# First attention of a sixteen-stage network: TensorE's order in groups of four units

## The chip, the cores and the metric

The kernel runs on one core of a Trainium2 chip. The metric is the device time of one execution in microseconds; lower is better. The core's engines run side by side, each with its own queue of instructions in a fixed order: TensorE (PE, matrix multiplications, with its weight loads shown as PEld), VectorE (DVE), ScalarE (ACT), GpSimd (POOL) and SyncE (SP, which issues most transfers). An instruction starts when those ahead of it in its queue and those whose results or buffers it needs are done. TensorE writes only to PSUM; VectorE and ScalarE copy from there into SBUF.

## The reference

The network has sixteen stages; each adds its result to x, of shape (4, 512, 128), after a layer normalisation. The change touches only the first, an attention with 16 heads of width 64:

```python
x = x + _L0_attn_a_ref(_layernorm(x), q_w, q_b, k_w, k_b, v_w, v_b, l_w, l_b)

def _L0_attn_a_ref(x, ...):
    q = jnp.einsum('bsd,hpd->bhsp', x, q_w) + q_b          # likewise k and v
    scores = jnp.einsum('bhqp,bhkp->bhqk', q, k) / jnp.sqrt(jnp.float32(P))   # P = 64
    attn = jax.nn.softmax(scores, axis=2)                  # over the queries, not the keys
    ctx = jnp.einsum('bhqk,bhkp->bqhp', attn, v)
    return ctx.reshape(B, S, H * P) @ l_w.T + l_b
```

The softmax runs over the queries. So the denominator belongs to a key, and can be put into that key's row of v.

## The kernel before

All data are fp32 and x stays in SBUF. The first stage, `L0a`, works through 4 batches of 8 head pairs, 32 groups `m`. A group has four *units* `n = 4m + j`, one for each block of 128 keys, with both heads of the pair.

For a unit, `scores(n)` (line 526) lets TensorE multiply 128 keys by 512 queries for each of the two heads (64 rows of the array each) into a PSUM tile of two banks, from a ring named "sc" of two such tiles. VectorE takes the two maxima `mx` over the queries (line 533); ScalarE takes two exponentials `e` with their sums (line 538), into a ring of nine SBUF buffers. After the fourth unit of a group VectorE takes the reciprocal `z` (line 547), and GpSimd multiplies v by it into `vz` (line 549). `sums(n)` (line 556) multiplies a unit's `e` by `vz` and adds it up over the four units of its group in a bank of the ring "ctx"; after the fourth, VectorE copies it out as `ct` (line 571).

The projections of a group each take one bank of a ring named "mm", which has two banks: `query(m)` (copied out, with bias and scale, by VectorE, line 507), `key(m)` (copied out with its bias by ScalarE, line 514), `value(b, c)` (one eighth of a batch's v; copied out with its bias by VectorE, line 524). `output(b, j)` (line 576) multiplies the eight finished `ct` of a batch by the last weights, also into "mm", and VectorE adds it to x and takes the moments for the next normalisation. The rings together fill the eight banks of PSUM: four for "sc", two for "mm", two for "ctx".

The order on TensorE is written out: every multiplication is pinned to program order. VectorE's and ScalarE's instructions stand in the order in which the same program names them. The loop at line 605 goes by pairs of units: scores of two units, sums of the two units six earlier (`LAG = 6`), then what `Plan` has set for this pair. That is query and key of the next group at one pair of each group, one value of the next batch at the other, and an output behind it four times a batch. `Plan.at(n, f, ...)` puts a call on step n, and `Plan.run(n)` makes the calls of that step in the order in which they were put there.

A short notation for blocks of TensorE's work: S, the scores of two units; C, the sums of two; Q, K, V, one projection each; O, one output. Before, a group is S C Q K, S C V, with O behind V where there is one.

Of the kernel before, what the change touches and what calls it, by code (L numbers as in the profile page):

```python
# [19 lines left out]
B, S, D = 4, 512, 128  # L20
NT = B * S
NC = NT // P
CB = S // P
# [251 lines left out]
class Net:  # L275
# [206 lines left out]
    def L0a(self):  # L482


        nc, tc = self.nc, self.tc
        LAG = 6
        with (
            tc.tile_pool(name="l0a_s", bufs=1) as sp,
            tc.tile_pool(name="l0a_r", bufs=3) as rp,
# [6 lines left out]
            plan = Plan()  # L496
# [29 lines left out]
            def scores(n):  # L526
                m, j = divmod(n, CB)
                sc = pp.tile([P, 2, S], F32, tag="sc", name="ps_s")
                for hh in range(2):
                    r = slice(64 * hh, 64 * hh + 64)  # L530
                    self.mm(sc[:, hh], k[m][r, j * P : j * P + P], q[m][r, :], pin=True)
                mx = rp.tile([P, 2], F32, tag="mx", name="mx", bufs=4)
                nc.vector.tensor_reduce(mx, sc, AX.X, ALU.max, negate=True)  # L533
                if j == 0:
                    z[m] = rp.tile([P, CB, 2], F32, tag="z", name="z")
                es[n] = rp.tile([P, 2, S], F32, tag="e", name="e", bufs=9)
                for hh in range(2):
                    nc.scalar.activation(  # L538
                        es[n][:, hh],
                        sc[:, hh],  # L540
                        AF.Exp,
                        bias=mx[:, hh : hh + 1],
                        accum_out=z[m][:, j, hh : hh + 1],
                    )
                if j == CB - 1:
                    b, pr = divmod(m, 8)
                    nc.vector.reciprocal(z[m], z[m])  # L547
                    vz[m] = rp.tile([P, CB, 2, 64], F32, tag="vz", name="vz")
                    nc.gpsimd.tensor_tensor(  # L549
                        vz[m],  # L550
                        v[b][:, :, pr * P : pr * P + P].rearrange("p j (h d) -> p j h d", h=2),
                        z[m].unsqueeze(3).to_broadcast([P, CB, 2, 64]),
                        ALU.mult,
                    )

            def sums(n):
                m, j = divmod(n, CB)
                if j == 0:
                    pc[m] = pp.tile([P, S], F32, tag="ctx", name="ps_c")
                for hh in range(2):  # L560
                    self.mm(
                        pc[m][64 * hh : 64 * hh + 64, :],
                        vz[m][:, j, hh],
                        es[n][:, hh],
                        start=j == 0,
                        stop=j == CB - 1,
                        pin=True,
                    )
                if j == CB - 1:
                    ct[m] = rp.tile([P, S], F32, tag="ct", name="ct", bufs=13)  # L570
                    nc.vector.tensor_copy(ct[m], pc[m])
                    if m % 8 == 7:
                        for i in range(CB):
                            plan.at(n + LAG + 1 + 4 * i, output, m // 8, i)

            def output(b, j):
                po = pp.tile([P, D], F32, tag="mm", name="ps_o")
# [16 lines left out]
            for c in range(8):  # L594
                value(0, c)
            for m in range(1, 8 * B):
                plan.at(4 * m - 4, query, m)
                plan.at(4 * m - 3, key, m)
            for b in range(1, B):
                for c in range(8):  # L600
                    plan.at(32 * (b - 1) + 4 * c + 2, value, b, c)
            for b in range(B):
                plan.at(32 * b + 16, self.bias_x, b, "a0_lb")

            for n in range(0, 32 * B + LAG + 16, 2):
                if n < 32 * B:
                    scores(n)
                    scores(n + 1)
                if 0 <= n - LAG < 32 * B:
                    sums(n - LAG)  # L610
                    sums(n - LAG + 1)
                plan.run(n)
                plan.run(n + 1)

    def experts(
        self, pools, NH, last, weighed, n, wide, gates, hidden, w2, rest, bias=False
# [7 lines left out]
        sp, rp, pp, dp = pools  # L624
        LAG = 12
        off = 64 if bias else 0
# [2292 lines left out]
```

## Time and profile before

| what | value |
|---|---|
| time, median of 3 runs | 2432.72 us (2425.2 to 2433.19) |
| profiled execution, from its first to its last instruction | 2427.6 us |
| TensorE busy over the span | 2172.0 us, 89% |
| first scores of the stage to its outputs' start | 26.7 to 380.8 us |
| TensorE busy from 26 to 381 us | 352.1 of 355 us |
| VectorE, ScalarE, GpSimd busy there | 229.4, 200.9, 33.3 us |
| granted TensorE clock there | 1.00 |

The page gives no other time of the profiled execution than its span. A line of the timeline begins with the start and the duration in microseconds; then come engine, line of the kernel, operation, output and inputs, shapes, and how many instructions are merged. In brackets stand the engine's idle time just before and what ended it. A matrix multiplication in fp32 shows as two MATMUL rows. The rows of TensorE overlap, since multiplications are pipelined, so a block's price is read from its start to the start of the next block.

### The profile page before, as it was taken

How to read it: one execution, taken by the hardware profiler on the slowest of the kernel's cores; microseconds unless marked ns; L12 is line 12 of the kernel's file. 1: busy time of each engine (PE TensorE's matmuls, PEld its weight loads, DVE VectorE, ACT ScalarE, POOL GpSimd, SP SyncE). 2: the span in 40 equal slices, each digit the busy share in tenths (PEclk: the TensorE clock that was granted, in tenths of full speed). 3: DMA queues.
4: the chain of work that ended last, by engine and by line, in shares of the span. 5: the costliest groups of instructions: out<-in, count | busy, mean ns of one | idle time of the engine just before them, and what ended most of it. 6: DMA issues, size and time to landing. Idle time of an engine off the chain costs nothing.

```text
span 2427.6 us, 32659 instructions
## 1 busy us (share of the span) xinstructions
PE 2172.0 (89%) x11639; PEld 1029.5 (42%) x11639; DVE 1727.7 (71%) x3413; ACT 1284.5 (53%) x2550; POOL 609.7 (25%) x443
## 2 busy tenths in 40 slices
PE   7999999999999998899876889888869998888868
PEld 2343334643334443568534446542214666422213
DVE  6666666589987775656465674678997657678995
ACT  4555555279845555343442454566655445467643
POOL 1100100010000001021153410038872014147871
PEclk9999999999899998999866989998979999988989
DMA  3000001300000000410200014334552520034550
GB/s 143 1 1 1 1 1 48 94 1 2 2 1 2 1 1 1 106 36 2 107 1 1 0 42 91 69 121 140 157 145 54 91 49 2 1 113 146 158 153 20
DMA packets 68882, 127.79 MB, mean 53 GB/s; under 512 B 9329, under 2 KB 29297, under 8 KB 68081
## 3 DMA queue, kind: packets, MB, share of 16 engines
q1 hardware_dynamic: 68720, 125.71, 19.2%
q8 instruction: 92, 1.51, 0.3%
q14 instruction: 70, 0.57, 0.1%
HBM read 119.91 MB, written 5.64 MB: 52 GB/s over the span
## 4 chain that ended last, share of the span: by engine, by line
PE 25%; DVE 12%; issue 8%; ACT 5%; DMA 1%; POOL 1%; SPq 0%; POOLq 0%; DVEq 0%; ACTq 0%
PE ps_o L346 6%; PE ps L346 4%; DVE hc L2361 3%; PE ps_x L346 2%; PE ps_g L346 2%; PE ps_du L346 2%; DVE ps_du L2356 2%; PE ps_y L346 1%; PE ps_h L346 1%; PE ps_s L346 1%; DMA wt<-dram 1%; DVE xn L393 1%; PE ps_d L346 1%; PE ps_tr L351 1%; ACT da L2342 1%
## 5 line engine op out<-in xcount | busy, mean ns | idle before, releaser
L2366 POOL TENSOR_TENSOR hc<-hc,cr 128x1024 f32<-128x1024 f32 x126 | 297.3, 2360 | 117.6 <-DVE hc L2361 111.6
L2361 DVE TENSOR_TENSOR_SCAN hc<-da,ps_du 128x1024 f32<-128x1024 f32 x128 | 290.9, 2274 | 0.0
L346 PE MATMUL ps_s<-k,q 32*128 32x512 f32 (+3 forms) x1088 | 277.5, 593 | 10.7 <-DVE mx L839 7.9
L538 ACT ACTIVATE e<-ps_s,mx 128x512 f32<-128x512 f32 x256 | 172.4, 685 | 139.5 <-DVE mx L533 132.9
L346 PE MATMUL ps_du<-du,spread 64*128 64x512 f32 x512 | 163.6, 711 | 63.3 <-DVE hc L2361 63.1
L925 DVE TENSOR_REDUCE nm<-ps_s 128x1 f32<-128x512 f32 x256 | 160.2, 681 | 60.3 <-PE ps_s L346 58.9
L2342 ACT ACTIVATE da<-da,am 128x512 f32<-128x512 f32 x248 | 165.7, 715 | 65.0 <-DMA da<-dram 49.0
L346 PE MATMUL ps<-xT,w_L2f 128*128 128x512 f32 (+1 forms) x416 | 193.4, 612 | 0.0
L1011 ACT ACTIVATE e<-ps_st 128x512 f32<-128x512 f32 x256 | 135.4, 602 | 93.8 <-PE ps_s L346 82.4
L533 DVE TENSOR_REDUCE mx<-ps_s 128x2 f32<-128x1024 f32 x128 | 150.9, 1218 | 43.9 <-PE ps_s L346 43.6
L2356 DVE TENSOR_TENSOR ps_du<-ps_du,br 128x1024 f32<-128x1024 f32 x128 | 154.8, 1210 | 30.5 <-PE ps_du L346 30.4
L346 PE MATMUL ps_st<-q,k 32*128 32x512 f32 x512 | 165.3, 625 | 1.7 <-DVE q L942 1.0
L850 ACT ACTIVATE e<-e,mx 128x512 f32<-128x512 f32 (+3 forms) x256 | 140.2, 549 | 19.3 <-DVE mx L839 18.6
L346 PEld LDWEIGHTS ps_s<-k,q 32*128 32x128 f32 x1088 | 99.2, 192 | 105.7 <-DVE mx L839 49.6
L346 PE MATMUL ps_s<-q,k 64*128 64x512 f32 x512 | 129.1, 618 | 2.2 <-ACT e L538 1.7
L346 PE MATMUL ps_c<-e,vz 128*64 128x512 f32 x512 | 123.5, 604 | 0.8 <-POOL vz L549 0.8
L1933 DVE SCALAR_TENSOR_TENSOR t<-ps,w_L2f,t 128x512 f32<-128x512 f32 (+1 forms) x104 | 76.6, 746 | 61.8 <-PE ps L346 38.9
L346 PEld LDWEIGHTS ps_du<-du,spread 64*128 64x128 f32 x512 | 46.2, 205 | 173.9 <-issue 113.8
L346 PEld LDWEIGHTS ps<-xT,w_L2f 128*128 128x128 f32 (+1 forms) x416 | 75.5, 190 | 95.8 <-issue 75.2
L549 POOL TENSOR_TENSOR vz<-v,z 128x512 f32<-128x512 f32 x32 | 33.3, 1042 | 323.1 <-DVE z L547 294.1
L839 DVE CUSTOM_DVE_ANT_0 e<-ps_s,tri 128x512 f32<-128x512 f32 (+3 forms) x256 | 109.5, 483 | 6.1 <-PE ps_s L346 6.1
L659 DVE TENSOR_TENSOR hc<-hc,wt 128x1024 f32<-128x1024 f32 x80 | 94.7, 1188 | 23.6 <-ACT hc L1936 12.1
(499 smaller groups left out, 4179.5 us busy)
## 6 DMA issues: line engine op xcount, KB each, us to landing
da<-dram SPq DMA_DIRECT2D x124, 256.0 KB
da<-dram SPq DMA_DIRECT2D x124, 255.5 KB
wt<-dram SPq DMA_DIRECT2D x144, 128.0 KB
wt<-dram SPq DMA_DIRECT2D x32, 256.0 KB
dram<-dl SPq DMA_DIRECT2D x16, 256.0 KB
wt<-dram SPq DMA_DIRECT2D x16, 224.0 KB
wt<-dram SPq DMA_DIRECT2D x16, 192.0 KB
wt<-dram SPq DMA_DIRECT2D x16, 160.0 KB
```

The lines of the kernel that those rows point to most:

```text
L346: i = self.nc.tensor.matmul(out, lhsT, rhs, start=start, stop=stop)
L533: nc.vector.tensor_reduce(mx, sc, AX.X, ALU.max, negate=True)
L538: nc.scalar.activation(es[n][:, hh], sc[:, hh], AF.Exp, bias=mx[:, hh : hh + 1], accum_out=z[m][:, j, hh : hh + 1],)
L659: nc.vector.tensor_tensor(h, h, wt[b, k][:, r:e], ALU.mult)
L839: red = nc.vector.tensor_tensor_reduce(e[:, i, :w], sc[i][:, :w], tri[:, S - w :], -1.0, BIG, ALU.add, ALU.min, mx[:, i : i + 1],)
L850: nc.scalar.activation(e[:, i, :w], e[:, i, :w], AF.Exp, bias=mx[:, i : i + 1], scale=-1.0, accum_out=z[:, i : i + 1],)
L925: nc.vector.tensor_reduce(nm[:, j, i, 9:10], sc, AX.X, ALU.max, negate=True)
L1011: keep(nc.scalar.activation(es_[n][:, i], sc, AF.Exp))
L2342: nc.scalar.activation(da[n][:, t, t:], src[:, t:], AF.Exp, scale=am[:, at : at + 1])
L2356: keep(nc.vector.tensor_tensor(dx[n], dx[n], br, ALU.mult))
L2361: keep(nc.vector.tensor_tensor_scan(h, a, x, 0.0, ALU.mult, ALU.add))
L2366: keep(nc.gpsimd.tensor_tensor(hc[n], hc[n], cr, ALU.mult))
```

## The change

The loop now goes by groups of four units. Each round issues scores of two units, then everything planned for this group (query and key of the next group, a value, an output, in this order), then scores of the other two units, then the sums of all four units of the group before. The plan's steps are counted in groups; `LAG` is gone.

```diff
-        LAG = 6
...
                     if m % 8 == 7:
                         for i in range(CB):
-                            plan.at(n + LAG + 1 + 4 * i, output, m // 8, i)
+                            plan.at(m + 2 + i, output, m // 8, i)
...
             for m in range(1, 8 * B):
-                plan.at(4 * m - 4, query, m)
-                plan.at(4 * m - 3, key, m)
+                plan.at(m - 1, query, m)
+                plan.at(m - 1, key, m)
             for b in range(1, B):
                 for c in range(8):
-                    plan.at(32 * (b - 1) + 4 * c + 2, value, b, c)
+                    plan.at(8 * (b - 1) + c, value, b, c)
             for b in range(B):
-                plan.at(32 * b + 16, self.bias_x, b, "a0_lb")
-
-            for n in range(0, 32 * B + LAG + 16, 2):
-                if n < 32 * B:
-                    scores(n)
-                    scores(n + 1)
-                if 0 <= n - LAG < 32 * B:
-                    sums(n - LAG)
-                    sums(n - LAG + 1)
-                plan.run(n)
-                plan.run(n + 1)
+                plan.at(8 * b + 4, self.bias_x, b, "a0_lb")
+
+            for m in range(8 * B + CB + 1):
+                if m < 8 * B:
+                    scores(4 * m)
+                    scores(4 * m + 1)
+                plan.run(m)
+                if m < 8 * B:
+                    scores(4 * m + 2)
+                    scores(4 * m + 3)
+                if 0 < m <= 8 * B:
+                    for j in range(CB):
+                        sums(4 * m - 4 + j)
```

A group is now S, Q K V, S, C C, with O behind V where there is one. No operation is added, dropped or resized. The values of the last three batches fall into groups 0 to 23; outputs fall into groups 9 to 12, 17 to 20 and 25 to 28, and the last four stand behind the loop's last sums.

## The prediction

> **What bounds the kernel now.** I read the page's busy rows and slices first, then the timeline of TensorE over one group of four units, then VectorE and ScalarE at the stage's start, then the two places of the stage where TensorE waits. From the page:
>
> ```profile
> PE 2172.0 (89%) x11639; PEld 1029.5 (42%) x11639; DVE 1727.7 (71%) x3413; ACT 1284.5 (53%) x2550; POOL 609.7 (25%) x443
> PE   7999999999999998899876889888869998888868
> PEclk9999999999899998999866989998979999988989
> ```
>
> TensorE leads. The changed stage runs from 26.7 us (first scores) to 380.8 us (last outputs); PE is at 9 there, and the table of stretches gives a granted clock of 1.00 for all of it, with DVE 229 and ACT 201 busy of 355 us. So only TensorE's order and its waits can move this stage. One group, on TensorE alone:
>
> ```profile
> 203.52 1.02 PE L346 MATMUL ps_k<-xT,w_L0a 128*128 128x512 f32 x2
> 204.47 1.99 PE L346 MATMUL ps_s<-q,k 64*128 64x512 f32 x8
> 206.39 1.94 PE L346 MATMUL ps_c<-e,vz 128*64 128x512 f32 x8
> 208.26 1.12 PE L346 MATMUL ps_v<-w_L0a,xT 128*128 128x512 f32 x2
> 209.31 1.99 PE L346 MATMUL ps_s<-q,k 64*128 64x512 f32 x8
> 211.23 1.94 PE L346 MATMUL ps_c<-e,vz 128*64 128x512 f32 x8
> 213.10 1.12 PE L346 MATMUL ps_q<-xT,w_L0a 128*128 128x512 f32 x2
> ```
>
> Start to start, S (scores of two units) costs 1.92, C (sums of two) 1.86, V 1.05, Q+K 1.91 us: 10.54 a group and no wait. What stands behind a score block is read at the stage's first S (start 26.73):
>
> ```profile
> 27.91 2.35 DVE L533 TENSOR_REDUCE mx<-ps_s 128x2 f32<-128x1024 f32 x2 [0.38 <-PE ps_s L346]
> 30.18 0.74 DVE L507 TENSOR_SCALAR q<-ps_q,w_L0a 128x512 f32<-128x512 f32 x1
> 31.17 0.69 ACT L538 ACTIVATE e<-ps_s,mx 128x512 f32<-128x512 f32 x1
> 31.83 0.70 ACT L514 ACTIVATE k<-ps_k,w_L0a 128x512 f32<-128x512 f32 x1
> ```
>
> The copy of q out of PSUM comes behind both maxima and ends 4.19 us after S began (30.92); the copy of k comes behind four exponentials and ends 5.80 after (32.53). Both are in PSUM ring "mm", which has two banks. What a TensorE block does that needs a bank of this ring still being copied is seen with the eight V at the start:
>
> ```profile
> 21.11 0.69 DVE L524 TENSOR_TENSOR v<-ps_v,rows 128x512 f32<-128x512 f32 x1 [0.35 <-PE ps_v L346]
> 21.86 0.30 PEld L346 LDWEIGHTS ps_v<-w_L0a,xT 128*128 128x128 f32 x2 [0.75 <-DVE v L524]
> ```
>
> It starts 0.06 us after the copy ends (21.80). Score banks ("sc", two) come free late too, where nothing stands between two S:
>
> ```profile
> 295.93 1.99 PE L346 MATMUL ps_s<-q,k 64*128 64x512 f32 x8
> 299.92 1.13 PE L346 MATMUL ps_s<-q,k 64*128 64x512 f32 x4
> 301.26 1.13 PE L346 MATMUL ps_s<-q,k 64*128 64x512 f32 x4 [0.21 <-ACT e L538]
> 302.32 1.94 PE L346 MATMUL ps_c<-e,vz 128*64 128x512 f32 x8
> ```
>
> That is 3.99 and 5.33 us after the earlier S began, 6.39 to the next block. Last, a block of four units' sums and the outputs (O):
>
> ```profile
> 309.89 2.05 PE L346 MATMUL ps_o<-w_L0a,ct 128*128 128x128 f32 x16
> 311.87 1.99 PE L346 MATMUL ps_s<-q,k 64*128 64x512 f32 x8
> 377.26 3.65 PE L346 MATMUL ps_c<-e,vz 128*64 128x512 f32 x16 [0.78 <-POOL vz L549]
> 380.84 7.41 PE L346 MATMUL ps_o<-w_L0a,ct 128*128 128x128 f32 x64
> ```
>
> O alone costs 1.98, four units' sums 3.58 (two C cost 3.72).
>
> **The change, part by part.** No matmul, copy or transfer is added or dropped. Blocks per group become S, Q K V (and O), S, C4. In the built kernel's order ScalarE, POOL and SP have the same sequence as before. VectorE has each pair of maxima still ahead of q's copy; V's copy moves ahead of the second pair, the copy of the context behind it.
>
> *Fewer switches of block.* C4 for two C saves 0.14. Q, K and V in one run, if nothing waits, save 0.20: V's 1.05 becomes the 0.85 of two 0.43 us passes (V to V at the start, 19.95 to 20.81). Together 0.34 a group with V.
>
> *New wait 1: V on q's copy.* Q, K and V take three turns of a ring of two, so V needs q's bank. Count from S. Q starts at 1.92, K at 2.88, V could at 3.73. q's copy ends at 4.19, so V starts at 4.25 and, having started from a standstill, costs 1.05: the second S starts at 5.30. Its banks have been free since 3.99 and (second unit, due at 6.26) 5.33. Then S 1.92 and C4 3.58: the group takes **10.80** against 10.54, +0.26. Queued behind V are the second S, C4 and everything after; nothing else of TensorE can pass.
>
> *New wait 2: O on k's copy.* Where an output follows V, it needs k's bank: 5.80 + 0.06 = 5.86. O 1.98, S 1.92, C4 3.58: **13.34**. Before, such a group took 12.32 (134.93 to 147.25, K to K): +1.02. Where it follows K without V (last batch), it waits for q's copy, 4.25 + 1.98 + 1.92 + 3.58 = **11.73** against 11.47 (315.65 to 327.12): +0.26.
>
> *Groups with neither V nor O.* S, then S on freed banks, next block at 6.39, C4 to **9.97**; before 10.18 (294.01 to 304.19): −0.21.
>
> *Start.* First sums come, as before, after the scores of eight units, but no C fills the gaps. First S 26.73; V waits to 30.98, second S 32.03; third S waits for score banks (32.03 + 3.99 = 36.02, second unit 37.36), ends 38.42; Q K; q's copy, behind the reciprocal (37.42) and two maxima, ends 40.51; V 40.57; fourth S 41.62; C4 43.54; third group at 47.12. Before, its S began at 44.08: +3.0.
>
> *End.* From S of the last group to the outputs: S, S on freed banks and C4 end at 9.97, but the last sums need vz, which before came 5.49 after the last unit's scores began (371.77 to 377.26): 5.33 + 5.49 + 3.58 = 14.40 against 14.71 (366.13 to 380.84): −0.3.
>
> *Edits costed at nothing.* V's copy now stands before the second pair of maxima: ready 1.16 after V began (5.41), done 6.10, maxima due at 6.48; without that 0.38 us of cover up to 0.69 a group would be lost. Reciprocal and copy of the context end 0.12 + 0.69 after C4, 0.37 before the next maxima are due (S + 1.18). vz is ready some 2 us into the next group and used at 7.2. At most eight units wait for their sums; of the nine e buffers, the one written next had its sums a group earlier. The four bias additions on POOL ran at 15.8 to 20.8 us, ahead of the stage's loop, and still can.
>
> *Sum.* Groups 2 to 30: 14 with V × 0.26 = +3.6; 8 with V and O × 1.02 = +8.2; 4 with O × 0.26 = +1.0; 3 plain × −0.21 = −0.6; start +3.0; end −0.3: **+14.9 us**. Bounds of the two prices that no row shows in this place: the start from a standstill costs V between 0.85 and 1.05 (22 × 0.2 = 4.4 less at most), and a wait costs from 0.06 to 0.2 us beyond the copy (the idle shown at 301.26) for 30 waits, 4 more. So +10.5 to +19; I take the rows' own starts, since V after a wait is shown at 1.05.
>
> The profiled execution spans 2427.6 us and no row lies outside it; the shown runs are 2425.2, 2432.7 and 2433.2, their median 5.1 above. 2432.7 + 14.9 = 2447.6. About 0.5% (12.2 us) is what a measurement of this kernel can tell from no change.
>
> [...]
>
> **The rivals.** *Not slower: the ring does not bind.* If q's copy ended by 3.67 after S, 0.52 earlier than shown (ahead of one maximum), and k's likewise, only the switches would count: 22 × −0.34 = −7.5; O without V −0.36 × 4 = −1.4; plain −0.6; start +2.0; end −0.3: −7.8, 2425. For it: TensorE has shown no wait for this ring in steady groups. Against: Q, K and V never came together there, and VectorE's order keeps both maxima ahead.
>
> *Smaller: O does not wait for k.* If ScalarE does k's copy before the second unit's exponentials, O runs on from V: 4.25 + 2.83 (V to S, 218.80 to 221.63) + 5.50 = 12.58, +0.26 in place of +1.02: +8.8, 2441. Against: the built order and the row at 31.83.
>
> *Larger: VectorE falls behind.* It does 4 × 1.21 + 0.75 + 0.69 + 0.69 + 0.19 = 7.2 us of each 10.8, but the margins are 0.37 and 0.38. If one is missed by 0.4 a group in 26 groups: +10 more, 2458. Against: both are counted from rows of the same order.
>
> **How the numbers follow.** Forecast 0.68 (own range 2443 to 2452), ring not binding 0.06, smaller 0.13, larger 0.13. Slower by over 0.5% (above 2444.9): the larger case and all but 0.05 of the forecast, 0.76. Faster (below 2420.6) needs more than the −7.8 of the first rival, a piece of it with run noise: 0.03. The rest, 0.21, is the same. The range leaves out the first rival and the top of the larger: 2437 to 2458.
>
> **What would show it.** Right: V's weight load waits for DVE q some 0.5 us, O's for ACT k some 0.5 us; group periods 10.8, 13.3, 11.7, 10.0; the stage's outputs begin near 396; the rest of the kernel unmoved. Wrong: Q, K, V in 2.8 us without a wait, periods near 10.2; or second S or maxima late by more than the sum has, for score banks or VectorE.

## The result, and the profile after

The changed kernel takes 2443.56 us (median of 5 runs, 2441.04 to 2446.07), the kernel before 2432.62 us beside it (5 runs): ratio 1.0055, 95% interval 1.0038 to 1.0072. By the medians it is slower by 10.9 us, by the ratio by 13.4 us: the ratio is not the quotient of the two medians, which is 1.0045, and the means of the five runs give 1.0058. Measured again beside the experiments it was slower by more, 1.0086 (1.0072 to 1.0101); both are taken up below. The profiled execution took 2442.09 us, with a span of 2440.0 us. One kernel below, with half of the first values later and two banks, was profiled in a run of 3645.18 us at a mean granted clock of 0.665, where its other four runs had 0.929 or more, so no profile of it is read and its time is the median of those four.

The page of the changed kernel, its busy times, and TensorE's slices:

```profile
PE 2165.6 (89%) x11639; PEld 1029.5 (42%) x11639; DVE 1728.1 (71%) x3413; ACT 1283.0 (53%) x2550; POOL 610.3 (25%) x443
...
PE   7999999999899998899885889988868998888868
```

Busy times and counts of instructions are nearly those of before, and the slices of the first 400 us read as before, one 7 and then 9. Nothing on this page tells that the stage got longer; a loss of half a microsecond in each group of eleven is lost in rounding. The timeline shows it: one group with a value, and one with a value and an output, on TensorE and with the copy that is waited for.

```profile
104.56 1.99 PE L346 MATMUL ps_s<-q,k 64*128 64x512 f32 x8
...
108.01 0.74 DVE L506 TENSOR_SCALAR q<-ps_q,w_L0a 128x512 f32<-128x512 f32 x1
108.80 1.13 PE L346 MATMUL ps_v<-w_L0a,xT 128*128 128x512 f32 x2 [0.34 <-DVE q L506]
...
115.36 1.99 PE L346 MATMUL ps_s<-q,k 64*128 64x512 f32 x8
...
126.16 1.99 PE L346 MATMUL ps_s<-q,k 64*128 64x512 f32 x8
...
130.41 1.12 PE L346 MATMUL ps_v<-w_L0a,xT 128*128 128x512 f32 x2 [0.34 <-DVE q L506]
131.33 0.70 ACT L513 ACTIVATE k<-ps_k,w_L0a 128x512 f32<-128x512 f32 x1
132.08 2.05 PE L346 MATMUL ps_o<-w_L0a,ct 128*128 128x128 f32 x16 [0.55 <-ACT k L513]
```

(Two lines fewer stand in the changed file, so the copy of q is L506 here, that of k L513, the exponentials L537.) V begins 4.24 us after its group's first S instead of 3.73, O 5.92 us after it, each 0.05 us behind the end of the copy. The waits of TensorE from 26 to 400 us, with total, number and longest:

```profile
PE ps_v L346 <- DVE q L506: 7.9, 23, 0.3
...
PE ps_o L346 <- ACT k L513: 4.3, 8, 0.5
PE ps_o L346 <- DVE q L506: 1.4, 4, 0.3
```

Before, 24 weight loads of V waited for the maxima (19.4 us in all, from 26 to 381 us), behind other work, and no matmul waited for a copy of q or k. Now 23 V wait for q's copy, 8 O for k's and 4 O for q's.

| part of the stage, us | before | after | difference | predicted |
|---|---|---|---|---|
| group with V | 10.54 | 10.80 | +0.26 (14 groups) | +0.26 |
| group with V and O | 12.32 | 13.40 | +1.08 (8) | +1.02 |
| group with O alone | 11.47 | 11.73 | +0.26 (4) | +0.26 |
| group with neither | 10.18 | 9.98 | −0.20 (3) | −0.21 |
| third group to last group's start | 322.05 | 335.27 | +13.2 | +12.2 |
| first S to the third group's start | 17.35 | 23.09 | +5.7 | +3.0 |
| last group's start to the outputs | 14.71 | 14.41 | −0.3 | −0.3 |
| stage, first S to outputs | 354.1 | 372.8 | +18.7 | +14.9 |
| outputs' successor (first `ps_g`) to the span's end | 2036.7 | 2029.7 | −7.0 | 0 |

The stage lost more than was predicted, by the start; the rest of the kernel, which the change does not touch, came out shorter in this one profile. The start, on TensorE, and the clock in a piece of it (after the stretch: its length, then busy time and number of instructions for PE, PEld, DVE, ACT and POOL, the granted clock, DMA):

```profile
36.70 1.13 PE L346 MATMUL ps_s<-q,k 64*128 64x512 f32 x4 [1.95 <-ACT e L537]
...
40.05 2.07 PE L346 MATMUL ps_q<-xT,w_L0a 128*128 128x512 f32 x2
```

```profile
36.00:38.00 2.00, 1.13 (x4) 0.30 (x4) 0.29 (x1) 1.99 (x6) 0.00 (x0) 0.93 0.00 0
38.00:40.00 2.00, 1.96 (x4) 0.51 (x4) 1.30 (x2) 0.64 (x2) 1.04 (x1) 0.50 0.00 0
...
44.00:46.00 2.00, 2.00 (x6) 0.49 (x6) 0.69 (x1) 0.55 (x1) 0.00 (x0) 0.86 0.00 0
```

The idle of 1.95 us before the third S is the predicted wait for the score banks. What was not predicted is that after it TensorE works at half its clock for a while: Q takes 2.07 in place of 1.13 us. The two stretches left out, from 40 to 44 us, have 0.50 as well, so the time at half clock follows from the clock column, with 1.00 and 0.50 taken as its only values: 2 × 2.00 × (1 − 0.93) + 2.00 + 2.00 + 2.00 + 2 × 2.00 × (1 − 0.86) = 6.84 us.

### The profile page after: what moved, and what is told of

Same layout as the page of the kernel before. It is cut to its first block, busy times and chain, and to the rows that moved or that the text cites. A ratio compares the mean times of both kernels' runs of the same rounds, so it can differ in the third digit from the quotient of the medians.

```text
span 2440.0 us, 32604 instructions
## 1 busy us (share of the span) xinstructions
PE 2165.6 (89%) x11639; PEld 1029.5 (42%) x11639; DVE 1728.1 (71%) x3413; ACT 1283.0 (53%) x2550; POOL 610.3 (25%) x443
## 4 chain that ended last, share of the span: by engine, by line
PE 25%; DVE 12%; issue 8%; ACT 4%; DMA 1%; POOL 1%; SPq 0%; POOLq 0%; DVEq 0%; ACTq 0%
PE ps_o L346 6%; PE ps L346 5%; DVE hc L2363 3%; PE ps_x L346 2%; PE ps_g L346 2%; DVE ps_du L2358 2%; PE ps_du L346 2%; PE ps_h L346 1%; PE ps_s L346 1%; PE ps_y L346 1%; DVE xn L393 1%; DMA wt<-dram 1%; PE ps_d L346 1%; PE ps_tr L351 1%; DVE ln_st L374 1%
## 5 line engine op out<-in xcount | busy, mean ns | idle before, releaser
L537 ACT ACTIVATE e<-ps_s,mx 128x512 f32<-128x512 f32 x256 | 172.6, 686 | 176.1 <-DVE mx L532 176.1
L346 PE MATMUL ps_c<-e,vz 128*64 128x512 f32 x512 | 116.9, 598 | 0.8 <-POOL vz L548 0.8
L661 DVE TENSOR_TENSOR hc<-hc,wt 128x1024 f32<-128x1024 f32 x80 | 94.7, 1189 | 25.6 <-ACT hc L1938 12.2
```

Source lines behind the costliest of these rows:

```text
L346: i = self.nc.tensor.matmul(out, lhsT, rhs, start=start, stop=stop)
L537: nc.scalar.activation(es[n][:, hh], sc[:, hh], AF.Exp, bias=mx[:, hh : hh + 1], accum_out=z[m][:, j, hh : hh + 1],)
L661: nc.vector.tensor_tensor(h, h, wt[b, k][:, r:e], ALU.mult)
```

## The experiments

Theory: the two banks of ring "mm" make V wait for q's copy and O for k's, and that is the whole steady loss. Rivals: it is the order itself (switches of block, VectorE, the score banks), or the start.

### A third bank for the projections, with the new order

The third bank is taken from "ctx", which keeps one, so that the three rings take eight banks as before.

```diff
-            tc.tile_pool(name="l0a_p", bufs=2, space=PSUM) as pp,
+            tc.tile_pool(name="l0a_p", bufs=3, space=PSUM) as pp,
...
-                sc = pp.tile([P, 2, S], F32, tag="sc", name="ps_s")
+                sc = pp.tile([P, 2, S], F32, tag="sc", name="ps_s", bufs=2)
...
-                    pc[m] = pp.tile([P, S], F32, tag="ctx", name="ps_c")
+                    pc[m] = pp.tile([P, S], F32, tag="ctx", name="ps_c", bufs=1)
```

> The changed kernel with the eight PSUM banks divided otherwise: three for the projections' ring "mm" and one for "ctx", in place of two and two. Nothing else differs. Theory (V and O wait for the copies of q and k because the ring has two banks): no wait before V or O; groups with V take 1.92 + 2.77 + 1.92 + 3.58 = 10.2 us (10.80 in the changed kernel), with V and O 12.05 (13.40), with O alone 11.1 (11.73), plain ones 9.98 as before; 14 x 0.6 + 8 x 1.35 + 4 x 0.6 + 1.2 at the start = 22 us less than the changed kernel, near 2421 us, 0.995 of the kernel before. Rival (the time was lost to VectorE's maxima, to score banks or to the start): periods stay 10.8 and 13.4, near 2443 us. If one bank for ctx binds, the sums' first multiplication waits for DVE ct and the groups grow.

Measured: 2426.22 us (11 runs) against 2430.81 (25), ratio 0.9981 (0.9970 to 0.9992). A group with V and O on TensorE:

```profile
130.61 1.99 PE L346 MATMUL ps_s<-q,k 64*128 64x512 f32 x8
...
134.35 1.02 PE L346 MATMUL ps_v<-w_L0a,xT 128*128 128x512 f32 x2
135.21 1.95 PE L346 MATMUL ps_o<-w_L0a,ct 128*128 128x128 f32 x16
...
142.58 1.99 PE L346 MATMUL ps_s<-q,k 64*128 64x512 f32 x8
```

V and O follow without a gap: V costs 0.86 us with O behind it (134.35 to 135.21), the group takes 11.97 in place of 13.40, and a group with V alone 10.19 in place of 10.80. With the waits gone the new order is the faster one, by the switches that it saves: the stage takes 348.4 us against 354.1 before. The steady loss is the ring's. The whole gains less than expected (2421 us, 0.995): from the third group to the last it takes 312.9 us in place of 322.05 before, but the start still costs 3.6 us more than before, a spell of half clock among it. The price of the single "ctx" bank is one wait of 0.89 us for `ct` at the very end, where 0.78 us for `vz` stood.

### The same rings with the old order

The same three lines, put into the kernel before.

> The kernel before with the same division of PSUM (three banks for "mm", one for "ctx"). Theory: in the old order no steady group waits for this ring, so groups stay at 10.54 and 12.32 us and the time within 0.1% (about 1 us less at most, from the eight values at the start). Rival (the third bank is worth something in any order): the old order gains some of the 22 us too.

Measured: 2432.56 us, ratio 1.0003 (0.9992 to 1.0015); groups of 10.54 and 12.32 us as before, stage 354.2 us. A third bank by itself is worth nothing. In the old order no matmul of the steady groups waits for a bank of "mm"; only order and ring together decide.

### The output in the other ring

To part the two waits, O alone is moved out of "mm"; V stays there.

```diff
-                po = pp.tile([P, D], F32, tag="mm", name="ps_o")
+                po = pp.tile([P, D], F32, tag="ctx", name="ps_o")
```

> The changed kernel, with the outputs' banks taken from the ring "ctx" in place of "mm"; V still waits for q. Theory (two separate waits): V's weight load still waits for DVE q, O no longer for ACT k: groups with V and O 12.6 us (13.40), with O alone 11.1 (11.73), with V 10.80 as they are; 8 x 0.8 + 4 x 0.6 = 9 us less than the changed kernel, near 2434 us. Rival (O is dear for itself, or waits for something else): 13.4 stays, 2443 us.

Measured: 2437.98 us (8 runs), ratio 1.0023 (1.0010 to 1.0036), and on TensorE:

```profile
124.30 1.99 PE L346 MATMUL ps_s<-q,k 64*128 64x512 f32 x8
...
128.55 1.12 PE L346 MATMUL ps_v<-w_L0a,xT 128*128 128x512 f32 x2 [0.34 <-DVE q L506]
129.51 1.95 PE L346 MATMUL ps_o<-w_L0a,ct 128*128 128x128 f32 x16
...
136.89 1.99 PE L346 MATMUL ps_s<-q,k 64*128 64x512 f32 x8
```

V waits as in the changed kernel, O no more. The group takes 12.59 us, which is the 12.58 that the rival "O does not wait for k" had; groups with V alone stay at 10.80, and a group with O alone falls from 11.73 to 11.12, as expected. The time is 4 us above the 2434 expected. So O's wait is worth 13.40 − 12.59 = 0.81 us in each of 8 groups, V's 12.59 − 11.97 = 0.62 in each of 22, its costlier start included.

### Key before query

> The changed kernel with key ahead of query in each group, so that V needs the bank of k, whose copy ends 1.6 us later than q's. Theory (the ring): V starts at 5.86 after the first scores in place of 4.25; groups with V 12.4 us (10.80), with V and O 14.2 (13.40, O then has q's bank, long free), with O alone 13.3 (11.73); 14 x 1.6 + 8 x 0.8 + 4 x 1.6 + 3 at the start = 38 us more, near 2482 us. Rival (V's delay has another cause than the copy two places earlier): no change, 2443 us.

```diff
-                plan.at(m - 1, query, m)
                 plan.at(m - 1, key, m)
+                plan.at(m - 1, query, m)
```

Measured: 2453.32 us, ratio 1.0092 (1.0076 to 1.0108). The first group with V after the start; ScalarE and TensorE in order of time:

```profile
46.26 1.99 PE L346 MATMUL ps_s<-q,k 64*128 64x512 f32 x8
...
50.04 0.69 ACT L513 ACTIVATE k<-ps_k,w_L0a 128x512 f32<-128x512 f32 x1
50.61 0.69 ACT L537 ACTIVATE e<-ps_s,mx 128x512 f32<-128x512 f32 x1
50.77 1.12 PE L346 MATMUL ps_v<-w_L0a,xT 128*128 128x512 f32 x2 [0.61 <-ACT k L513]
...
57.33 1.99 PE L346 MATMUL ps_s<-q,k 64*128 64x512 f32 x8
```

The direction holds: the projection that comes first names the copy that V waits for, here k's. The size does not: 2482 us was expected. The group takes 11.07 us (later ones mostly 11.13) where about 12.4 was expected, because ScalarE's order moved with the edit: the copy of k now stands ahead of the second unit's two exponentials instead of behind them. It begins 3.78 us after S, and V 0.04 us after its end. A group with V and O falls to 12.92 us, since O no longer waits. In turn the second unit's exponentials come later, and a group with neither V nor O grows to 10.56 us, on a longer wait for a score bank. The edit changed two engines' orders, not one, which the expectation had missed. The program still names all four exponentials ahead of `key`: only TensorE's multiplications are pinned, and unlike what the section on the kernel before says, ScalarE does not always follow the program's order. What chose this order is not shown.

### Half of the first values later

The start's gap of 1.95 us has nothing to fill it. Here four of the eight values that stand ahead of the first S are moved behind the second scores of the first two groups.

```diff
-            for c in range(8):
-                value(0, c)
+            fill = Plan()
+            for c in range(0, 8, 2):
+                value(0, c)
+                fill.at(c // 4, value, 0, c + 1)
...
                     scores(4 * m + 3)
+                fill.run(m)
```

> The changed kernel, with four of the first batch's eight values (those of pairs 4 to 7, needed from group 4 on) taken out of the run ahead of the loop and put behind the second scores of groups 0 and 1, two each. They fill the 1.95 us in which TensorE stands before group 1. Theory (the start costs more than its waits, since TensorE's granted clock halves after this gap): the gap shrinks to some 0.2 us, and with it the spell of clock 0.50 (37.9 to 44.7 us in the changed kernel, some 2.7 us of time) goes; third group 2 us earlier by the gap and up to 2.7 more by the clock; groups after it as in the changed kernel (10.80, 13.40). Rival (the spell comes at that time of the kernel whatever TensorE does): only the 2 us, and clock 0.50 still there near 38 to 45 us.

Measured: 2444.85 us (4 runs), ratio 1.0064 (1.0049 to 1.0078), beside 1.0086 for the changed kernel on the same chip, so about 2429.1 × 0.0022 = 5.3 us less, with intervals that overlap. That the half clock goes with the gap, which this run was to test, is not shown by it; what the moved values do to the start is read from the next kernel.

### Three banks and the late values

Both edits together.

> Ring of three and late values together, meant as the version that beats both kernels: periods 10.2, 12.0, 11.1, 9.98 as with the ring of three, and 2 us less at the start, with a half-clock spell up to 4: some 2423 us, 0.996 to 0.997 of the kernel before. Rival: the late values' copies on VectorE delay the maxima of groups 0 and 1, and the start gains nothing: 0.998.

Measured: 2423.40 us (12 runs) against 2429.10 (17), ratio 0.9971 (0.9959 to 0.9983): faster than both kernels, as expected (0.996 to 0.997). From the kernel with three banks alone (0.9981) it can't be told apart by time. Its start:

```profile
29.40 1.98 PE L346 MATMUL ps_v<-w_L0a,xT 128*128 128x512 f32 x4
31.42 1.13 PE L346 MATMUL ps_s<-q,k 64*128 64x512 f32 x4
```

The two values take the place of the 1.95 us of idle, and the clock stays at 1.00 from 26 to 50 us; that it stays there because the idle is gone is not shown by one profile, since it stayed full behind the idle too (see the changed kernel again, below). From first S (22.79) to the third group (44.00) it takes 21.21 us and contains four values more, two by two at 1.92 us (38.50 to 40.42 for the second two); so 17.4 for the rest, the 17.35 of before.

### The value beside query and key, in the old order

The other half of the change: the kernel before, with its pairs and its sums in between, but V at the pair of Q and K.

```diff
-                    plan.at(32 * (b - 1) + 4 * c + 2, value, b, c)
+                    plan.at(32 * (b - 1) + 4 * c + 1, value, b, c)
```

> The kernel before, with its loop by pairs, and one part of the change alone: the value moved from its own pair to behind query and key, so that groups are S C Q K V, S C. Theory (V, where it stood, also covered the wait for score banks): V waits some 0.16 us for q's copy, saves one switch (0.2), and the two S with only C between them now wait for exponentials, 3.99 and 5.33 us after the earlier S: groups with V 11.3 us (10.54), the 8 with an output in that place little changed (12.3), 14 x 0.7 = 10 us more, near 2441 us. Rival (only the number of switches counts): 0.2 less a group, near 2428 us.

Measured: 2442.63 us, ratio 1.0058 (1.0044 to 1.0072). A group on TensorE, and the score banks' waits in the stage:

```profile
40.23 1.99 PE L346 MATMUL ps_s<-q,k 64*128 64x512 f32 x8
...
45.50 1.13 PE L346 MATMUL ps_s<-q,k 64*128 64x512 f32 x4 [0.21 <-ACT e L538]
...
49.39 1.02 PE L346 MATMUL ps_k<-xT,w_L0a 128*128 128x512 f32 x2
50.40 1.12 PE L346 MATMUL ps_v<-w_L0a,xT 128*128 128x512 f32 x2
51.46 1.99 PE L346 MATMUL ps_s<-q,k 64*128 64x512 f32 x8
```

```profile
PE ps_s L346 <- ACT e L538: 6.2, 21, 1.9
```

Q, K and V come together here too, and V's wait all but goes. With C ahead of Q the maxima are done, and what VectorE's copy of q waits for is Q itself (29 times, 10.3 us in all); Q ends at 49.55 us. V, whose weight loads wait for that copy (24 times, 20.0 us in all), begins 1.01 us after K (49.39 to 50.40) in place of 0.86 in a run without a wait: 0.15 us late, as expected (0.16), and not the 0.51 of the changed kernel. The loss is another one. With V gone from between the two S, only C is left there, the score banks are late, and the group takes 11.23 us here and 11.29 in most others (11.3 expected), against 10.54. Of these 0.75 us, 0.69 stand at the two S (85.42 to 91.81 less C's 1.86 and two S at 1.92), and 0.06 at Q, K and V. A group with V and O takes 12.58 us where 12.3 was expected. So V's old place was cover for the score banks, and what makes V wait long in the changed kernel is not that the three are together but that they come straight behind S, with q's copy behind two maxima.

### The changed kernel again

> The changed kernel unaltered, once more beside these on the same chip: between the two profiles its first stage is longer by 18.7 us and its whole by 12.4. Theory (the rest of the kernel is the same, and its time varies with the spells of half clock): the stage repeats within 3 us, the rest of the kernel after the first ps_g lies anywhere in the 2030 to 2047 us that the profiles showed so far, and the ratio to the kernel before is 1.006 to 1.008. Rival (the later stages really run faster behind the changed stage): rest again near 2030 and ratio 1.005 or less.

Measured: 2448.58 us (2446.03 to 2454.27), ratio 1.0086 (1.0072 to 1.0101), groups of the same lengths as in its first profile. The start, and a pair of scores near the stage's end:

```profile
35.40 1.13 PE L346 MATMUL ps_s<-q,k 64*128 64x512 f32 x4 [1.95 <-ACT e L537]
...
385.70 3.42 PE L346 MATMUL ps_s<-q,k 64*128 64x512 f32 x8 [2.01 <-ACT e L537]
```

The same idle of 1.95 us, and the clock stays full (1.00 from 26 to 50 us; Q takes 1.12): first S (26.16) to third group takes 20.26 us, +2.9 against before. This time the half clock comes behind the idle of 2.01 us in the last group, whose scores take 3.42 us:

```profile
386.00:388.00 2.00, 2.00 (x6) 0.50 (x4) 0.77 (x1) 0.98 (x4) 0.00 (x0) 0.58 0.00 0
388.00:390.00 2.00, 2.00 (x8) 0.43 (x6) 1.29 (x2) 1.45 (x4) 0.00 (x0) 0.56 0.00 0
```

From the last group's S (381.70) to the outputs (397.06) it takes 15.36 us, 0.65 more than before in place of 0.3 less. The stage takes 370.9 us: 2.9 + 13.2 + 0.65 = 16.8 more than before.

## Why the prediction was right

2447.6 us was predicted, +14.9, with bounds of +10.5 and +19; measured were +10.9 and, the second time, +19.5 by the medians, one on each side. The terms of the steady groups, 12.2 of the 14.9 us (13.2 measured), were right in mechanism and nearly in size. That the first total lies as near as it does is partly luck: in the first pair of profiles the start lost 2.7 us more than its term and the untouched rest of the kernel ran 7.0 us shorter, two misses of opposite sign. Term by term:

- **V on q's copy.** Right in cause and size: V due at 3.73 us, starting at 4.24 (4.25 predicted), then costing 1.06. The timeline's rows named it as predicted. Three banks take the wait away and the group falls to 10.19, where the rival "ring does not bind" had 10.54 − 0.34 = 10.20.
- **O on k's copy.** Right; the size was 0.06 us low (13.34 against 13.40, 8 × 0.06 = 0.5 us), since O began 5.92 us after S instead of 5.86. The experiment with O in the other ring shows the two waits to be separate, at the predicted 12.58.
- **Groups with O alone, and with neither.** 11.73 and 9.98, as worked out. The four kinds give 14 × 0.26 + 8 × 1.08 + 4 × 0.26 − 3 × 0.20 = 12.7 of the 13.2 us that the steady groups lost; the other 0.5 is before's own, whose groups from the third on took 322.05 us where its four kinds sum to 322.5.
- **The start.** Right by mechanism, and in the second profile by size (+2.9 against +3.0). In the first it was +5.7. The term did not allow for the clock: in the first profile the idle of 1.95 us was followed by 6.84 us at half clock, in the second by none, and 2.8 us came of it (23.09 against 20.26 us in the two profiles of the same kernel). That the idle itself would be there was in the sum (third S at 36.02; 36.70 measured, with first S 0.73 later).
- **The end.** −0.3 without a spell of half clock, as predicted; +0.65 with one. The outputs began at 400.2 and 397.1 us, where near 396 was predicted.
- **Edits costed at nothing.** None shows a cost. VectorE's margins were 0.37 us (v's copy ends at 110.66, maxima begin at 111.03) and 0.36 us (`ct` copied at 105.37, maxima at 105.73), as counted, so the rival "VectorE falls behind" is out:

```profile
109.97 0.69 DVE L523 TENSOR_TENSOR v<-ps_v,rows 128x512 f32<-128x512 f32 x1 [1.22 <-PE ps_v L346]
111.03 2.36 DVE L532 TENSOR_REDUCE mx<-ps_s 128x2 f32<-128x1024 f32 x2 [0.38 <-PE ps_s L346]
```

- **The rest of the kernel unmoved.** In the first pair of profiles it was 7.0 us shorter after the change (2029.7 against 2036.7), in the second profile 2036.9. In all these profiles it ran from 2029.7 to 2047.3 us with no edit there, longest (old order with three banks) at a mean granted clock of 0.929 for the whole span and shortest at 0.938. That spells of half clock in the later stages make this spread is supported by the clock: by an estimate that takes 1.00 and 0.50 as its only values, a span of 2440.0 us at 0.938 was at half clock for 303 us, before's 2427.6 us at 0.934 for 320, and the longest, 2436.0 us at 0.929, for 346. The order in between is not exact (2040.3 us at 0.935 with three banks), and what starts the spells there was not traced. With this spread, the stage's +18.7 stands in spans that differ by 12.4 us, and its +16.8 in spans that differ by 16.4; the medians, +10.9 and +19.5, are of other runs as well. The sum of the terms with full clock, 2.9 + 13.2 − 0.3 = 15.8 us, is what the change costs at full clock; the half clock that followed an idle came on top, 2.8 us at the start of one profile and about 1 us at the end of the other.

The price of V from a standstill was also right, 1.06 us, but the ground given for it was not in the rows: they show 1.05 for V behind C, and in the run of eight V one that began 0.06 us after a copy (21.86) was followed 0.86 us later (22.72). The experiments show the parts: without a wait V costs 0.86 us with O behind it and 0.95 with S behind it (three banks, 51.03 to 51.98), after a wait 0.96 and 1.06. By these four figures the standstill cost some 0.1 us here and the switch to S as much again. A matmul that waited for a copy began 0.04 us (V at 50.77, key before query) to 0.06 us (V at 21.86, the kernel before) after it.

## What to carry to other kernels

Before blocks of work are put together to save switches, count the turns of the PSUM ring that they take in a row, and for each turn beyond the ring's size compare when the block is due with when the copy of the oldest one ends on its engine, queue included. The same reordering lost 16.8 and 18.7 us in this stage with two banks and gained 5.7 with three, and the third bank alone gained nothing: order and buffers are one decision. And look at what the moved block covered in its old place: V between two pairs of scores was the time in which their banks came free (groups of 10.54 us with it there, mostly 11.29 without).

## What the hardware showed that was not expected

**Half clock after a short idle.** TensorE's idle of 1.95 us before the third S is the same in the changed kernel's two profiles and in those of the experiments with three banks, O in the other ring, key before query, and V beside query and key. In three of the six the granted clock then fell to 0.50, in three it stayed at 1.00. By the clock column, worked out as above, the half clock lasted 6.84 us in the first profile of the changed kernel, 3.4 with three banks (0.60 and 0.55 in two stretches of 2 us), 3.4 with O in the other ring (0.77, 0.50, 0.87), and 3.4 at the end of the second profile (0.58, 0.56). Each of these is 3.4 us or twice that. A longer idle, of 2.01 us, stands before the second scores of the last group in six profiles: the changed kernel's two, three banks with and without the late values, O in the other ring, and key before query. It was followed by half clock in one, the changed kernel's second, where those scores took 3.42 us; in the other five they took 1.13 us for each unit and the sums behind them 3.65 us, as at full clock. So of twelve idles of 1.95 or 2.01 us, four were followed by half clock. Their length does not tell these four from the other eight, and what does is not shown.

**Order of one engine by an edit on another.** Putting the key's projection ahead of the query's moved ScalarE's copy of k past two exponentials: it begins 3.78 us after S, against 5.17 in the changed kernel (131.33, with S at 126.16), where it stands behind all four. An order that TensorE is pinned to is not the only one that the program's text sets.
